# A graph network's second layer: relation rows made where they are used, operands read from PSUM, and puts that do not wait for each other

## The chip, the cores and the metric

The kernel runs on one NeuronCore of a Trainium2 chip. Its engines each work through a queue of their own: TensorE (PE; its weight loads are shown as PEld), VectorE (DVE), ScalarE (ACT), GpSimd (POOL) and SyncE (SP), with DMA transfers issued from several of these queues. The metric is device time in microseconds for one execution of the whole program, and lower is better. The kernel before took 3470.16 us, the median of nine runs that lay between 3455.51 and 3485.51.

## The reference

A graph has 3125 nodes with 256 features and 53125 edges (25000 drawn, each in both directions, and a self loop per node). Every edge has one of 64 types and a weight. The network has two layers, each followed by a feed-forward part with routing. Cut to what matters (L is a layer norm without scale; `W`, `b` are different for every place):

```python
xn = L(x)
# layer 0: weighted sum over neighbours, and a linear-attention "mixer"
x = x + segment_sum(xn[src] * w[:, None], dst) @ W.T + b + mixer0(xn)
# feed-forward 0: one of 32 experts for each node, by the largest logit
x = x + experts32(L(x))
# layer 1: attention over edges, with a row for each edge type
xn = L(x)
Q, K, V = heads(xn + 0.1 * query_emb)                 # 4 heads of 64
s  = einsum('ehd,ehd->eh', Q[dst], K[src] + 0.2 * rel_w[type][:, None, :]) / 8
a  = segment_softmax(s, dst)
out = segment_sum(a[:, :, None] * V[src], dst) @ Wo + bo
x = x + (L(out + xn) * gamma + beta) + mixer1(xn)
# mixer 1: 4 heads of 32; context = softmax(k over nodes)^T v; out = (q context) @ W_out + b_out
# feed-forward 1: a small graph attention gives 4 scores for each node;
# the two best of 4 experts are mixed
x = x + top2_of_4(L(x))
```

## The kernel before

The nodes are sorted by the number of their edges and cut into 25 tiles of 128 rows. Row p of a tile has one node, and its edges lie in slots: tile t has `SLOTS[t]` of them, from 38 down to 10, 444 in all. The source rows of a slot, one for each of the 128 nodes, are fetched by one indirect DMA (a gather) that GpSimd writes descriptors for. The residual `xs` stays in SBUF for all 25 tiles.

The code is written with tiles and pools. A pool has a number of buffers for each name, and a tile that takes a buffer waits for the readers of the one that had it before. The order in which an engine works through its instructions is set by a planner when the program is built, from the modelled readiness of each instruction; within `tc.manual_schedule(engines=...)` the named engines keep the order in which the program is written.

`layers()` (from L1675) holds both layers:

- `front()` (L1469) has layer 0 and the first half of layer 1. It prepares the edges, runs the first mixer over 25 tiles (`first_mixer`, L1368), then goes through seven groups of up to four tiles. For each tile, `slots` (L1341) gathers the neighbours' rows (L1351), weights and adds them on VectorE (L1357), and multiplies the sum by the layer's weights. `relation_rows` (L1311) then makes the row of `0.2 * rel_w[type]` for each slot: for four slots at a time VectorE writes a one-hot of the types (L1321), TensorE transposes two slots at once (L1327), ScalarE copies that to SBUF (L1329), TensorE multiplies it by the table in three bf16 parts (L1333), ScalarE copies the result to SBUF (L1336) and SP stores it in DRAM (L1338). After the four tiles come the 32 experts (`experts`, L1571: matmuls L1583, L1584 and L1588, activations L1586) and `projections` (L1601): keys and values of each tile are scattered to a DRAM table `kvtab` by node (L1619, on GpSimd), the layer-normed row and the query go to a DRAM table `own` (L1622, on SP), the second mixer's query goes transposed into `qT`, which is one half of the tile `kq` (L1626), and the mixer's context is summed up.
- `source_lists()` (L1221) scatters, in 256 DMAs of GpSimd (L1230), lists that the router will use.
- The second mixer's outputs are made for all 25 tiles one after the other (L1716 to L1720): two matmuls each into PSUM, and an add into `xs` on VectorE.
- The second layer's loop (L1725 to L1870) goes over the tiles. `scores(t)` loads `own` into `xq` (L1732) and the tile's relation rows into `rr` (L1734), and for each group of four slots has four gathers of 2 KB rows of keys and values from `kvtab` (L1742), then VectorE adds the relation rows to the keys (L1748), multiplies by the query (L1750) and sums over each head (L1751). A softmax over the slots follows (L1754 to L1763). `values(t)` weights the values, mostly on ScalarE by head (L1779) and for every fourth slot on VectorE (L1776), and TensorE sums them in PSUM by products with the identity (L1781). The gathers have 14 buffers of four slots. `project` (L1784) works one tile behind: it multiplies by the output weights and adds `xn` (L1791). After every five tiles, `norms` (L1841) adds to `xs`, and `router_rows` (L1806) makes the router's 20 numbers for each node and scatters them into a DRAM table (L1833).
- `routed_by_slots()` (L1893) is the last feed-forward part: gathers of 20 numbers for each node and each neighbour (L1910 and L1943), attention over them, gates, the four experts on TensorE (L2070 and L2082), adds into `xs` (L2101) and the puts of the tiles to the output by node, one indirect DMA each (`put`, L2104 to L2106). ScalarE, VectorE and GpSimd are in written order here.

Of the kernel before, what the change touches and what calls it, by code (L numbers as in the profile page):

```python
# [12 lines left out]
F32 = mybir.dt.float32  # L13
BF16 = mybir.dt.bfloat16
I32 = mybir.dt.int32
AF = mybir.ActivationFunctionType
OP = mybir.AluOpType
# [4 lines left out]
P = 128  # L22
N = 3125
D = 256
KB = D // P
NT = 25
# [870 lines left out]
class Fast(Net):  # L897
# [395 lines left out]
    def relations(self, ctx):  # L1293
        nc, a = self.nc, self.a
        HD, NR = 64, 64
        keep = ctx.enter_context(self.tc.tile_pool(name="rel_keep", bufs=1, reuse_waits="tile"))
# [14 lines left out]
    def relation_rows(self, pool, ps, t):  # L1311

        nc = self.nc
        HD, NR = 64, 64
        S = SLOTS[t]
        S2 = S + S % 2
        tab = self.dram.tile([P, S, HD], F32, name=f"rel{t}")
        for g in range(0, S2, 4):
            n = min(4, S2 - g)
            oh = pool.tile([P, 4, NR], BF16, name="oh")  # L1320
            nc.vector.tensor_tensor(  # L1321
                oh[:, :n], self.iota[:, None, :NR].to_broadcast([P, n, NR]),
                self.typs[t][:, g:g + n].unsqueeze(2).to_broadcast([P, n, NR]), op=OP.is_equal)
            po = ps.tile([P, 2, P], BF16, name="pg")
            ohT = pool.tile([P, 2, P], BF16, name="ohT")
            for i in range(n // 2):
                nc.tensor.transpose(po[:, i, :], oh[:, 2 * i:2 * i + 2, :].rearrange("p i r -> p (i r)"),  # L1327
                                    self.identb)
            nc.scalar.copy(ohT[:, :n // 2], po[:, :n // 2])  # L1329
            pr = ps.tile([P, 4, HD], F32, name="pg")  # L1330
            for i in range(n // 2):
                for k in range(3):
                    nc.tensor.matmul(pr[:, 2 * i:2 * i + 2, :], ohT[:, i, :], self.relb[:, k],  # L1333
                                     start=(k == 0), stop=(k == 2))
            rr = pool.tile([P, 4, HD], F32, name="rr")
            nc.scalar.copy(rr[:, :n], pr[:, :n])  # L1336
            n = min(n, S - g)
            nc.sync.dma_start(tab[:, g:g + n, :], rr[:, :n])  # L1338
        self.rels.append(tab)

    def slots(self, t, ep, eps, w_y):  # L1341
# [18 lines left out]
        both = eps.tile([P, 2, D], F32, name="sums")  # L1360
# [108 lines left out]
    def front(self, kq, kvtab, own):  # L1469
# [5 lines left out]
        with ExitStack() as ctx:  # L1475
# [6 lines left out]
            self.relations(ctx)  # L1482
# [7 lines left out]
            with ExitStack() as mctx:  # L1490
                self.first_mixer(mctx, kq, nq, kvo)
# [739 lines left out]
```

## Time and profile before

| what | us |
|---|---|
| median of nine runs | 3470.16 |
| the profiled execution | 3466.32 |
| its span on the core | 3464.4 |
| preparation | 0 to 100 |
| first mixer | 100 to 600 |
| groups of tiles with gathers | 600 to 1105 |
| the remaining groups, and the second mixer's outputs from 1943 | 1105 to 1981 |
| the loop's gathers | 1932 to 2697 |
| end of the loop, last part of the router's numbers | 2697 to 2773 |
| router and its experts | 2773 to 3421 |
| the last puts | 3421 to 3464 |

The stages overlap, and the bounds were read from the timeline. The mean granted clock of TensorE was 0.757 of full speed. "Busy" is the time in which an instruction ran on an engine; a group's line has its busy time, the mean in ns of one, the idle time of the engine just before its instructions, and what ended most of that. "issue" means that the profile shows nothing that the engine waited for. In a timeline, each line has start, duration, engine, source line and operation, and in brackets the idle time before it.

### The profile page before, as it was taken

What the parts mean: (1) busy time and instruction counts of PE and PEld (TensorE: products, weight loads), DVE (VectorE), ACT (ScalarE), POOL (GpSimd) and SP (SyncE); (2) the same over time, 40 slices, a digit from 0 to 9 for tenths busy, and PEclk for the clock granted to TensorE, in tenths of its full rate; (3) what the DMA queues carried; (4) which work ended last, traced back from release to release, by engine and by line L of the source; (5) the groups of instructions that cost most, each with busy time, mean ns of one, the idle gap of its engine ahead of it and who ended that gap; (6) DMA issues with size and microseconds to landing.
All of it is one profiled execution on the core that took longest, in us unless ns stands there. A gap on an engine that the chain in (4) does not pass through costs nothing. (4 is left out here: it accounts for less than half of the span.)

```text
span 3464.4 us, 25978 instructions
## 1 busy us (share of the span) xinstructions
PE 1977.0 (57%) x7293; PEld 1169.9 (34%) x7293; DVE 1389.1 (40%) x4121; ACT 902.3 (26%) x2670; POOL 1692.6 (49%) x1675
## 2 busy tenths in 40 slices
PE   0266676656657828466484615445556543865774
PEld 0134343333434414233242313233333322532443
DVE  7356566746633101111102355668668401111124
ACT  0023233112202201111011025456456511321230
POOL 3564544464362070513416177778777274455422
PEclk9977787777777969778595657667576665987887
DMA  3333323433232000000000255666676210000001
GB/s 119 119 97 97 92 90 102 156 107 116 74 94 67 21 22 10 25 0 25 1 12 13 76 164 175 190 199 198 196 214 188 91 29 5 17 12 7 11 6 37
DMA packets 142407, 283.68 MB, mean 82 GB/s; under 512 B 39826, under 2 KB 79750, under 8 KB 141868
## 3 DMA queue, kind: packets, MB, share of 16 engines
q0 software_dynamic: 82656, 196.67, 20.1%
q1 hardware_dynamic: 51340, 77.01, 6.5%
q10 hardware_dynamic: 8256, 8.23, 0.8%
q8 instruction: 61, 1.00, 0.1%
q14 instruction: 94, 0.77, 0.1%
HBM read 243.47 MB, written 38.31 MB: 81 GB/s over the span
## 5 line engine op out<-in xcount | busy, mean ns | idle before, releaser
L1351 POOL DMA_INDIRECT g<-xtab,src x444 | 452.6, 1019 | 421.9 <-issue 117.1
L1742 POOL DMA_INDIRECT kv<-kvtab,src x444 | 532.3, 1199 | 192.8 <-issue 159.4
L1781 PE MATMUL pu<-kv,ident 128*128 128x256 f32 x888 | 318.1, 505 | 252.2 <-ACT kv L1779 217.5
L1943 POOL DMA_INDIRECT ed<-htab,nb x279 | 264.7, 949 | 271.3 <-issue 177.0
L1779 ACT ACTIVATE kv<-kv,sc 128x64 f32<-128x64 f32 x1372 | 340.9, 335 | 147.4 <-DVE sc L1763 72.7
L1781 PEld LDWEIGHTS pu<-kv,ident 128*128 128x128 f32 x888 | 193.9, 245 | 364.4 <-ACT kv L1779 298.5
L1588 PE MATMUL po<-w,h 128*128 128x256 f32 x800 | 227.0, 429 | 155.2 <-ACT h L1586 143.4
L1230 POOL DMA_INDIRECT gl<-gsrc,sidx x256 | 248.6, 971 | 79.5 <-issue 77.5
L1619 POOL DMA_INDIRECT kvtab<-kv,pid x25 | 24.3, 973 | 531.4 <-DVE kv L1616 519.8
L2082 PE MATMUL po<-w,h 128*128 128x256 f32 x800 | 212.6, 406 | 105.7 <-issue 105.1
L2070 PE MATMUL ph<-xT,w 128*128 128x512 f32 (+1 forms) x448 | 199.2, 597 | 50.1 <-ACT h L2072 25.7
L1588 PEld LDWEIGHTS po<-w,h 128*128 128x128 f32 x800 | 158.5, 210 | 201.4 <-ACT h L1586 167.6
L1583 PE MATMUL ph<-xT,w 128*128 128x512 f32 (+1 forms) x448 | 211.8, 600 | 0.0
L1748 DVE TENSOR_TENSOR kv<-kv,rr 128x1024 f32<-128x1024 f32 (+3 forms) x121 | 136.3, 1129 | 185.9 <-DMA kv<-kvtab,src 165.8
L2082 PEld LDWEIGHTS po<-w,h 128*128 128x128 f32 x800 | 155.9, 200 | 156.7 <-issue 139.9
L1357 DVE SCALAR_TENSOR_TENSOR acc<-g,wt,acc 128x256 f32<-128x256 f32 x419 | 196.3, 475 | 18.4 <-DMA g<-xtab,src 12.3
L1586 ACT ACTIVATE h<-ph,b 128x512 f32<-128x512 f32 (+1 forms) x112 | 71.9, 642 | 500.5 <-PE ph L1584 358.3
L2070 PEld LDWEIGHTS ph<-xT,w 128*128 128x128 f32 x448 | 86.7, 207 | 147.4 <-issue 103.5
L1750 DVE TENSOR_TENSOR kv<-kv,xq 128x1024 f32<-128x1024 f32 (+3 forms) x121 | 134.8, 1124 | 0.1
L1751 DVE TENSOR_REDUCE sc<-kv 128x16 f32<-128x1024 f32 (+3 forms) x121 | 134.2, 1119 | 0.1
L2072 ACT ACTIVATE h<-ph,b 128x512 f32<-128x512 f32 (+1 forms) x112 | 69.1, 641 | 204.2 <-PE ph L2070 136.5
L1321 DVE TENSOR_TENSOR oh<-iota,typ 128x256 bf16<-128x256 f32 (+1 forms) x121 | 48.3, 401 | 178.4 <-PE pg L1327 116.6
(432 smaller groups left out, 3144.8 us busy)
## 6 DMA issues: line engine op xcount, KB each, us to landing
dr<-in_gat_dst_row SPq DMA_DIRECT2D x32, 512.0 KB
rel<-rr SPq DMA_DIRECT2D x101, 128.0 KB
g<-xtab,src POOLq DMA_INDIRECT x444
kv<-kvtab,src POOLq DMA_INDIRECT x444
own<-xq SPq DMA_DIRECT2D x25, 256.0 KB
xq<-own SPq DMA_DIRECT2D x25, 256.0 KB
ed<-htab,nb POOLq DMA_INDIRECT x279
w<-in_ex_w ACTq DMA_DIRECT2D x2, 2048.0 KB
```

What stands on the lines that cost most here:

```text
L1230: ins = nc.gpsimd.indirect_dma_start(out=self.gl[:, :], out_offset=bass.IndirectOffsetOnAxis(ap=self.sidx2[:, c:c + 1], axis=0), in_=self. ...
L1351: nc.gpsimd.indirect_dma_start(out=g[:, s % 4, :], out_offset=None, in_=self.xtab[:, :], in_offset=bass.IndirectOffsetOnAxis(ap=self.srcs[ ...
L1357: nc.vector.scalar_tensor_tensor(acc, g[:, s % 4, :], self.wts[t][:, s:s + 1], acc, op0=OP.mult, op1=OP.add)
L1583: nc.tensor.matmul(ph[:, :n], w1[:, k, mc], xT[:, k, :n], start=(k == 0), stop=False)
L1588: nc.tensor.matmul(pos[j // 2][:, j % 2], h[:, j * P:(j + 1) * P], w2[:, m, :], start=False, stop=(m == M - 1 and (j % 2 == 1 or j == w - 1)))
L1742: nc.gpsimd.indirect_dma_start(out=kv[:, j, :], out_offset=None, in_=kvtab[:, :], in_offset=bass.IndirectOffsetOnAxis(ap=self.srcs[t][:, g ...
L1748: nc.vector.tensor_tensor(k4, k4, rr[:, g:g + n].unsqueeze(2).to_broadcast([P, n, 4, HD]), op=OP.add)
L1779: nc.scalar.activation(v[:, h * HD:(h + 1) * HD], v[:, h * HD:(h + 1) * HD], AF.Copy, scale=sc[:, s, h:h + 1])
L1781: nc.tensor.matmul(pu, self.ident, v, start=(s == 0), stop=(s == SLOTS[t] - 1))
L1943: nc.gpsimd.indirect_dma_start(out=ed[:, s, :], out_offset=None, in_=self.htab[:, :], in_offset=bass.IndirectOffsetOnAxis(ap=self.nbrs[t][ ...
L2070: nc.tensor.matmul(ph[:, :w], w1[:, e, k, m * P:(m + 1) * P], xT[:, :len(ts), k, :], start=(k == 0), stop=(k == KB - 1))
L2082: nc.tensor.matmul(po[:, i], hs[i][:, m, j * P:(j + 1) * P], w2[:, e0 + i, m, :], start=False, stop=(i == 1 and m == M - 1))
```

## The change

Eight things are changed.

1. `relation_rows` is taken out of `front()` and called inside `scores(t)`, for eight slots at a time. Its result stays in PSUM (`pr`, two buffers), and VectorE reads it there. The copy `rr` on ScalarE, the DRAM tables `rel` and their stores and loads go.
2. The query is copied by ScalarE to a PSUM tile `q`, and VectorE's product reads it there.
3. The second mixer's output of a tile is made in `project`, into a second half of `pz`, with an add of its own into `xs`. `qT` is now a tile of its own that lives on; the first mixer's `q2T` has another. The mixer's weights and the relation table are loaded ahead of `front()`.
4. The PSUM pool of the loop has one buffer for each name, and two for `q`, `pr` and `pu`. `sums` in `slots` has two.
5. The router's numbers are made after 5, 10, 15, 20, 23 and 25 tiles, where it was every five.
6. In `routed_by_slots`, GpSimd's order is left to the planner.
7. The puts are declared independent of each other.
8. The scratch memory for the descriptors of dynamic DMAs is set to 4096, where it had its default.

```diff
-    def relation_rows(self, pool, ps, t):
+    def relation_rows(self, pool, ps, t, g):
...
-        for g in range(0, S2, 4):
-            n = min(4, S2 - g)
-            oh = pool.tile([P, 4, NR], BF16, name="oh")
...
-            rr = pool.tile([P, 4, HD], F32, name="rr")
-            nc.scalar.copy(rr[:, :n], pr[:, :n])
-            n = min(n, S - g)
-            nc.sync.dma_start(tab[:, g:g + n, :], rr[:, :n])
-        self.rels.append(tab)
+        n = min(8, SLOTS[t] + SLOTS[t] % 2 - g)
+        oh = pool.tile([P, 8, NR], BF16, name="oh")
+        nc.vector.tensor_tensor(
+            oh[:, :n], self.iota[:, None, :NR].to_broadcast([P, n, NR]),
+            self.typs[t][:, g:g + n].unsqueeze(2).to_broadcast([P, n, NR]), op=OP.is_equal)
+        pt = ps.tile([P, 4, P], BF16, name="pT")
+        ohT = pool.tile([P, 4, P], BF16, name="ohT")
+        for i in range(n // 2):
+            nc.tensor.transpose(pt[:, i, :], oh[:, 2 * i:2 * i + 2, :].rearrange("p i r -> p (i r)"),
+                                self.identb)
+        nc.scalar.copy(ohT[:, :n // 2], pt[:, :n // 2])
+        pr = ps.tile([P, 8, HD], F32, name="pr", bufs=2)
+        for i in range(n // 2):
+            for k in range(3):
+                nc.tensor.matmul(pr[:, 2 * i:2 * i + 2, :], ohT[:, i, :], self.relb[:, k],
+                                 start=(k == 0), stop=(k == 2))
+        return pr
...
-        both = eps.tile([P, 2, D], F32, name="sums")
+        both = eps.tile([P, 2, D], F32, name="sums", bufs=2)
...
-                    self.relation_rows(ep, eps, t)
...
-                kq = one.tile([P, KB, NP], F32, name="kq")
-                self.front(kq, kvtab, own)
+                q2T = one.tile([P, KB, NP], F32, name="q2T")
+                self.front(q2T, qT, kvtab, own)
...
-                    for t in range(NT):
-                        po = ps.tile([P, D], F32, name="pk")
-                        nc.tensor.matmul(po, qT[:, t * P:(t + 1) * P], cw, start=True, stop=False)
-                        nc.tensor.matmul(po, self.ones3, b_mo, start=False, stop=True)
-                        nc.vector.tensor_add(self.xs[:, t, :], self.xs[:, t, :], po)
...
-                    rr = ep.tile([P, S0, HD], F32, name="rr")
-                    nc.sync.dma_start(rr[:, :S], self.rels[t])
+                    q = ps.tile([P, D], F32, name="q", bufs=2)
+                    nc.scalar.copy(q, xq[:, :D])
...
+                        if g % 8 == 0:
+                            rr = self.relation_rows(ep, ps, t, g)
+                        r0 = g % 8
...
-                            k4, k4, rr[:, g:g + n].unsqueeze(2).to_broadcast([P, n, 4, HD]), op=OP.add)
-                        nc.vector.tensor_mul(k, k, xq[:, None, :D].to_broadcast([P, n, D]))
+                            k4, k4, rr[:, r0:r0 + n].unsqueeze(2).to_broadcast([P, n, 4, HD]), op=OP.add)
+                        nc.vector.tensor_mul(k, k, q[:, None, :].to_broadcast([P, n, D]))
...
-                    pz = ps.tile([P, D], F32, name="pz")
-                    self.mm_rows(pz, uT, w_o, b_o)
-                    nc.vector.tensor_add(z, xq[:, D:], pz)
+                    pz = ps.tile([P, 2, D], F32, name="pz")
+                    self.mm_rows(pz[:, 0], uT, w_o, b_o)
+
+                    nc.tensor.matmul(pz[:, 1], qT[:, t * P:(t + 1) * P], cw, start=True, stop=False)
+                    nc.tensor.matmul(pz[:, 1], self.ones3, b_mo, start=False, stop=True)
+                    nc.vector.tensor_add(z, xq[:, D:], pz[:, 0])
+                    nc.vector.tensor_add(self.xs[:, t, :], self.xs[:, t, :], pz[:, 1])
...
+                parts = [range(a0, b0) for a0, b0 in zip((0, 5, 10, 15, 20, 23), (5, 10, 15, 20, 23, 25))]
...
-                engines={mybir.EngineType.Activation, mybir.EngineType.DVE, mybir.EngineType.Pool}))
+                engines={mybir.EngineType.Activation, mybir.EngineType.DVE}))
...
+                if puts:
+                    tc.declare_no_dep(ins, group="out", reason="other nodes")
+                tc.add_to_no_dep_group("out", ins)
+                puts.append(t)
...
-    nc = bacc.Bacc("TRN2", target_bir_lowering=False, num_devices=1)
+    nc = bacc.Bacc("TRN2", target_bir_lowering=False, num_devices=1, dynamic_dma_scratch_size=4096)
```

## The prediction

> **What bounds the kernel now.** I read the busy shares first, then the busy time by stretch, then the costliest groups, the waits, the chain that ended last, and the timelines of GpSimd and VectorE where the loop begins.
>
> The page's shares and granted clock:
>
> ```profile
> span 3464.4 us, 25978 instructions
> PE 1977.0 (57%) x7293; PEld 1169.9 (34%) x7293; DVE 1389.1 (40%) x4121; ACT 902.3 (26%) x2670; POOL 1692.6 (49%) x1675
> ```
>
> No engine is the bound of the whole, so it goes by stage. The stretches are: first mixer, two tile groups with gathers, five groups without, the second layer's loop, its end, the router with its experts, the tail. Columns: us, then busy time and count of PE, PEld, DVE, ACT, POOL, then clock, DMA share, GB/s.
>
> ```profile
> 100.00:600.00 500.00, 295.85 (x1437) 174.81 (x1438) 282.25 (x1131) 132.83 (x400) 256.02 (x254) 0.79 0.34 102
> 600.00:1105.00 505.00, 307.16 (x1499) 187.98 (x1498) 270.33 (x1028) 96.38 (x232) 253.77 (x250) 0.77 0.34 106
> 1105.00:1935.00 830.00, 502.03 (x1684) 281.01 (x1684) 108.42 (x351) 120.97 (x271) 268.45 (x301) 0.78 0.05 17
> 1935.00:2697.00 762.00, 393.76 (x1143) 239.58 (x1143) 486.51 (x792) 357.13 (x1373) 562.78 (x473) 0.66 0.61 182
> 2697.00:2773.00 76.00, 45.09 (x152) 28.79 (x152) 37.71 (x89) 39.44 (x152) 11.54 (x10) 0.72 0.24 77
> ```
>
> In front TensorE leads with 59 to 61% busy. In the loop it is GpSimd: 562.8 of 762 us in descriptor writing alone, and each gather is followed by a gap of 0.30 us (444 x 0.30 = 133 us), together 696. The groups:
>
> ```profile
> L1742 POOL DMA_INDIRECT kv<-kvtab,src x444 | 532.3, 1199 | 192.8 <-issue 159.4 <-ACT kv L1779 16.6 <-PE pu L1781 5.2
> L1327 PE MATMUL pg<-identb,oh 128*128 128x128 bf16 x229 | 37.2, 245 | 120.6 <-issue 73.4 <-ACT rr L1336 42.8 <-DVE oh L1321 2.9
> L1333 PE MATMUL pg<-self.relb,ohT 128*128 128x128 bf16 x687 | 69.2, 238 | 34.6 <-ACT ohT L1329 14.2 <-remote 12.0 <-issue 4.6
> L1336 ACT COPY rr<-pg 128x256 f32<-128x256 f32 (+1 forms) x121 | 43.8, 362 | 223.6 <-remote 100.7 <-PE pg L1333 59.9 <-issue 27.9
> ```
>
> A gather alone takes 0.95 us. The timelines show what stretches it: one that starts beside L1748, an add of two operands in SBUF, takes 1.94; and the second gather buffer came only when the last L1720 of the second mixer was done, after 43.97 us.
>
> ```profile
> 2206.01 1.22 DVE L1748 TENSOR_TENSOR kv<-kv,rr 128x1024 f32<-128x1024 f32 x1 [2.27 <-DMA kv<-kvtab,src]
> 2206.11 1.94 POOL L1742 DMA_INDIRECT kv<-kvtab,src  x1 [0.30 <-issue]
> ...
> 2217.03 0.95 POOL L1742 DMA_INDIRECT kv<-kvtab,src  x1 [0.30 <-issue]
> ...
> 1980.57 0.42 DVE L1720 TENSOR_TENSOR xs<-xs,pk 128x256 f32<-128x256 f32 x1 [1.05 <-PE pk L1719]
> ...
> 1980.95 1.99 POOL L1742 DMA_INDIRECT kv<-kvtab,src  x1 [43.97 <-issue]
> ```
>
> The tail, by the chain that ended last and the timeline: the last adds end near 3421, then puts to the output run one after the other, each waiting until the one before has landed.
>
> ```profile
> 3419.67 0.39 issue
> 3420.06 3.28 DMA out<-xs,pid
> ...
> 3436.81 0.96 POOL L2106 DMA_INDIRECT out<-xs,pid  x1 [2.21 <-DMA out<-xs,pid]
> 3459.11 0.96 POOL L2106 DMA_INDIRECT out<-xs,pid  x1 [2.21 <-DMA out<-xs,pid]
> ```
>
> **The sum's base** is the profiled execution: 3466.3 us, of which 3464.4 is span and 1.9 lies around it. The median of nine runs is 3470.2, 0.1% above; no change under about 0.3% can be told from none.
>
> **Front, relation rows out: -55 (0 to -150).** Gone are 229 transposes and 687 matmuls (37.2 + 69.2 = 106 us of TensorE), 121 one-hots (48.3 us of VectorE), two copies a group on ScalarE (43.9 + 43.8) and 101 stores on SP. TensorE is busy about 0.6 of these stages, and the small matmuls were often filling gaps, so I count half of the 106: 53, and 2 for the copies in TensorE's way. At 0, other work sets the pace: the gathers L1351 (452.6 us busy) or the chain of the experts hides it all. At most, 106 plus L1336's 44: 150.
>
> **Second mixer into the loop: -44 of GpSimd's start.** Its 50 matmuls (30.2 us) and 25 adds (10.4 at 415 ns, as L1791) no longer stand between the projections and the loop. The gathers start at 1936 and need not wait until 1981: 44 us. The work itself lies in project(), where TensorE is half idle. If the buffer waits for another owner of that memory instead, 0.
>
> **VectorE reads PSUM: -86 on GpSimd (0 to -111).** 444 gathers x (1.199 - 0.95) = 111 us is the stretch. Laid over VectorE's instructions, the gathers that met only L1751, with one input, took 949 ns mean, only reads of PSUM 960, only L1750 1674. With rows and query in PSUM both two-input operations become of the first kind. I leave 25 us of stretch for L1776, the one-hots and the softmax, whose inputs stay in SBUF. At 0, the stretch is from any long VectorE operation. VectorE itself gains or loses nothing: 256 wide from SBUF and PSUM, L1791 took 414 ns, L1776 415. [...]
>
> **What the loop gets: +60 of that back.** VectorE: 67 one-hots of 512 elements at about 0.62 (L1321's 401 ns for 256, extrapolated) = 42, on 486: 528. ScalarE: 25 query copies x 0.37 and 67 copies x 0.59 (L1165's 512 wide) = 49, on 357: 406. TensorE: 106 on 394: 500. SP loses 25 loads of rows. GpSimd: 444 x 1.25 = 555, 25 of stretch, 25 table scatters and 16 list gathers at about 1.3 = 54: 634. So GpSimd stays the longest, but its margin over the chain shrinks: each chunk of eight slots has one-hot, transposes, copy, matmuls before its first L1748, and these queue on TensorE behind the matmuls L1781 (which wait 217.5 us for ScalarE) and on ScalarE behind 335-ns products L1779. I take a third of the 155 us given to TensorE and ScalarE, about 52, and 8 for single-buffered PSUM, as path. The ends are 0 (hidden) and +270 (67 chunks x 4 us, all exposed: one-hot 0.6, four transposes of 37.2/229 = 0.16, copy 0.6, twelve matmuls of 69.2/687 = 0.10, together 3.0, and 1 for the hand-offs between engines). Loop: 44 + 86 - 60 = **-70**, from 765 to about 695.
>
> **Last router part of two tiles: -8.** From norms at 2745 to the first router gather at 2773.7 is 29 us; of the five table scatters (2760.3 to 2768.0) three go earlier, 5 us, and 3 of normalising.
>
> **Puts without the wait: -37.** The last add ends at 3421, the last put starts at 3459.1; with nothing to wait for it starts near 3421.7. Only if the adds came later is there less to win. **Free POOL order and 4096 of scratch: 0** (order: ±10, GpSimd idles 53% of the router stage; scratch: up to four gathers were in flight at once in the loop, a price as a rival).
>
> Sum: -55 - 70 - 8 - 37 = -170, **3296**.
>
> **Rival 1: the loop gives nothing.** The chunks' chains are exposed: 528 + 270 = 798 us of VectorE instead of 765, +33. For it: VectorE already waits 165.8 us for gathers and lags 25 us at the end; TensorE waits behind L1781. Against: the one-hots depend on nothing in the loop and rows have two buffers. -55 + 33 - 8 - 37 = -67: about 3400.
>
> **Rival 2: TensorE becomes the loop's bound, slower.** 916 matmuls and as many weight loads more: some eight more 16-KB loads of code (13 to 21) in a stage where the clock is 0.66. Each cost about 3 us of TensorE's "issue" time there (42 for 13); while GpSimd issues back to back in the router stage, one matmul of 0.59 us came every 2.80. At 17 us a code load, 500 + 357 = 857: +95, and front gives 30 only: +95 - 30 - 8 - 37 = +20, **3486**. It decides from a loop of about 840 on; below it the case is rival 1. Against: 1143 matmuls went through 762 us with 394 busy.
>
> **Rival 3: the small scratch makes GpSimd wait** for landings. The latency of a gather is 3.4 us median; if 1 in 28 of 1614 DMAs waits one latency, 58 x 3.4 = 197: -170 + 197 = +27. Against it only that no more than four were in flight; it needs a wait every 28th, and shows as gaps regular on GpSimd.
>
> **How the numbers follow.** Forecast 0.62, rival 1 0.25, rivals 2 and 3 together 0.11, nothing at all 0.02. Low end: front -110, loop -115 (GpSimd alone, 650), -8, -37 = -270: 3196, say 3200. High end: rival 1 with 20 more, 3420. The forecast's own range is 3230 to 3350. Faster: 0.62 + 0.25 = 0.87; same 0.02; slower 0.11.
>
> **What the profile after would show.** Gathers L1742's successor at 0.95 to 1.0 mean instead of 1.199 (else the PSUM step is wrong); the first wait of 44 us gone; loop about 695; no rr copies; the puts 1.3 us apart; front's stages some 55 shorter in all. Wrong it is if VectorE's add waits for the row matmuls (rival 1), if TensorE's idle in the loop is mostly "issue" (rival 2), or GpSimd shows waits on its own landings (rival 3).

## The result and the profile after

The changed kernel takes 3701.6 us (median of ten runs), the kernel before beside it 3472.3: a ratio of 1.067, 95% interval 1.065 to 1.070. The forecast was 0.95 and the range ended at 3420 us.

Runs of this study fell on chips of two kinds. On some the kernel before takes 3470 to 3504 us, as here; on others it takes 2782 to 2794. I call them the first and the second kind; the name says how a chip behaved in these runs, and whether it always does was not tried. Each ratio compares runs on one and the same chip, and on the second kind the changed kernel has 1.003. Of the distance from the forecast 0.95 to the measured 1.067, about half (0.064) thus came with the first kind of chip, and the other half (0.053) is in the kernel on either.

The profiled execution after has a span of 3681.2 us, before 3464.4. Its page, and the busy time by stretch (us, then PE, PEld, DVE, ACT, POOL, then clock, DMA share, GB/s; the stretches are those shown of before, cut where the loop's gathers now begin and end, from the groups without gathers on):

```profile
span 3681.2 us, 25500 instructions
PE 2012.3 (55%) x7293; PEld 1184.0 (32%) x7293; DVE 1385.4 (38%) x4071; ACT 870.2 (24%) x2520; POOL 1573.8 (43%) x1675
```

```profile
1105.00:1909.00 804.00, 478.93 (x1437) 262.53 (x1435) 92.41 (x295) 101.64 (x206) 266.37 (x298) 0.77 0.04 12
1909.00:2898.00 989.00, 455.98 (x1926) 290.68 (x1926) 489.86 (x809) 383.11 (x1430) 455.02 (x474) 0.65 0.43 126
2898.00:3025.00 127.00, 69.03 (x287) 44.64 (x287) 71.87 (x142) 53.88 (x191) 10.65 (x11) 0.67 0.11 37
```

The gathers begin at 1909 instead of 1932, 23 us earlier. They take 989 us instead of 765, though VectorE's work is the same (490 and 487 us) and GpSimd's fell from 563 to 455: no engine is busy for half of the stretch. From the first gather of the loop to the first gather of the router, which I call the loop from here on, it is 1116 us after and 841 before. What follows takes 656 instead of 691. With the span, -23 + 275 - 35 = +217, which is the whole difference.

The groups of the loop after:

```profile
L1731 POOL DMA_INDIRECT kv<-kvtab,src x444 | 426.2, 960 | 501.0 <-ACT kv L1768 375.0 <-issue 109.8 <-PE pu L1770 6.4
L1737 DVE TENSOR_TENSOR kv<-kv,pr 128x1024 f32<-128x1024 f32 (+3 forms) x121 | 133.4, 1124 | 335.2 <-remote 264.2 <-PE pr L1329 30.9 <-PE pT L1323 29.6
L1325 ACT COPY ohT<-pT 128x512 bf16<-128x512 bf16 (+3 forms) x67 | 34.8, 519 | 282.6 <-remote 207.6 <-PE pT L1323 59.7 <-issue 10.8
```

The gathers' mean is 960 ns, down from 1199: that step did what was forecast. But GpSimd stands 375 us waiting for buffers that ScalarE's products L1768 have still to work on, and VectorE's add waits 335 us for its rows. 264 of these end as "remote": the profile finds no instruction whose end let it go. The timeline shows what that means:

```profile
2275.74 0.56 ACT L1325 COPY ohT<-pT 128x512 bf16<-128x512 bf16 x1
2276.75 0.83 PE L1329 MATMUL pr<-self.relb,ohT 128*128 128x128 bf16 x12
2277.42 0.28 PE L1323 MATMUL pT<-identb,oh 128*128 128x128 bf16 x2
2277.57 0.95 POOL L1731 DMA_INDIRECT kv<-kvtab,src  x1 [0.30 <-issue]
...
2286.07 0.37 ACT L1775 COPY u<-pu 128x256 f32<-128x256 f32 x1 [9.77 <-remote]
...
2295.11 0.94 POOL L1731 DMA_INDIRECT kv<-kvtab,src  x1 [0.30 <-issue]
2300.08 2.35 DVE L1737 TENSOR_TENSOR kv<-kv,pr 128x1024 f32<-128x1024 f32 x2 [30.06 <-remote]
2300.20 0.37 ACT L1325 COPY ohT<-pT 128x256 bf16<-128x256 bf16 x1 [13.76 <-remote]
```

By the records TensorE has made the rows and the next transposes by 2277.7 us. ScalarE's copy of the sums starts 8 us later, VectorE's add and the copy of the transposes 22 us later, 4 us after the last of GpSimd's gathers. Until then the two engines do nothing but that one copy of the sums. Laying all such waits over GpSimd's work (rows of eight or more DMAs less than 0.6 us apart, together 1916 of 3681 us): of 788 us in which VectorE's waits end as "remote", 690 lie in such rows and 770 in them or within 5 us after; of ScalarE's 892 us, 755 and 865. The rows with their 5 us make up 2185 us, 59% of the span, and hold 98 and 97% of these waits. On the other kind of chip no view of the same program shows a wait that ends as "remote".

The puts at the end no longer wait for landings but, most of them, for the adds:

```profile
3674.09 0.98 POOL L2101 DMA_INDIRECT out<-xs,pid  x1 [0.36 <-DVE xs L2096]
3676.04 0.96 POOL L2101 DMA_INDIRECT out<-xs,pid  x1 [0.97 <-DVE xs L2096]
```

### The profile page after: what moved, and what is told of

Same layout as the page of the kernel before. It is cut to its first block, busy times and chain, and to the rows that moved or that the text cites. A ratio compares the mean times of both kernels' runs of the same rounds, so it can differ in the third digit from the quotient of the medians.

```text
span 3681.2 us, 25500 instructions
## 1 busy us (share of the span) xinstructions
PE 2012.3 (55%) x7293; PEld 1184.0 (32%) x7293; DVE 1385.4 (38%) x4071; ACT 870.2 (24%) x2520; POOL 1573.8 (43%) x1675
## 5 line engine op out<-in xcount | busy, mean ns | idle before, releaser
L1731 POOL DMA_INDIRECT kv<-kvtab,src x444 | 426.2, 960 | 501.0 <-ACT kv L1768 375.0
L1343 POOL DMA_INDIRECT g<-xtab,src x444 | 444.0, 1000 | 395.2 <-issue 117.7
L1770 PE MATMUL pu<-kv,ident 128*128 128x256 f32 x888 | 297.1, 478 | 166.8 <-ACT kv L1768 141.1
L1768 ACT ACTIVATE kv<-kv,sc 128x64 f32<-128x64 f32 x1372 | 333.6, 334 | 63.9 <-DVE sc L1752 44.2
L1770 PEld LDWEIGHTS pu<-kv,ident 128*128 128x128 f32 x888 | 178.8, 228 | 276.2 <-ACT kv L1768 221.2
L1737 DVE TENSOR_TENSOR kv<-kv,pr 128x1024 f32<-128x1024 f32 (+3 forms) x121 | 133.4, 1124 | 335.2 <-remote 264.2
L1577 ACT ACTIVATE h<-ph,b 128x512 f32<-128x512 f32 (+1 forms) x112 | 71.9, 642 | 538.7 <-PE ph L1575 384.1
L1329 PE MATMUL pr<-self.relb,ohT 128*128 128x128 bf16 x687 | 75.0, 284 | 191.5 <-ACT ohT L1325 146.0
L1739 DVE TENSOR_TENSOR kv<-kv,q 128x1024 f32<-128x1024 f32 (+3 forms) x121 | 133.4, 1122 | 0.1
L1582 DVE SCALAR_TENSOR_TENSOR xs<-po,xs 128x256 f32<-128x256 f32 x25 | 9.4, 416 | 327.1 <-PE po L1579 326.8
```

The costliest lines, as they stand in the source:

```text
L1343: nc.gpsimd.indirect_dma_start(out=g[:, s % 4, :], out_offset=None, in_=self.xtab[:, :], in_offset=bass.IndirectOffsetOnAxis(ap=self.srcs[ ...
L1731: nc.gpsimd.indirect_dma_start(out=kv[:, j, :], out_offset=None, in_=kvtab[:, :], in_offset=bass.IndirectOffsetOnAxis(ap=self.srcs[t][:, g ...
L1737: nc.vector.tensor_tensor(k4, k4, rr[:, r0:r0 + n].unsqueeze(2).to_broadcast([P, n, 4, HD]), op=OP.add)
L1768: nc.scalar.activation(v[:, h * HD:(h + 1) * HD], v[:, h * HD:(h + 1) * HD], AF.Copy, scale=sc[:, s, h:h + 1])
L1770: nc.tensor.matmul(pu, self.ident, v, start=(s == 0), stop=(s == SLOTS[t] - 1))
```

## Experiments

The chip's kind is given by the kernel before beside the run. "Late" is VectorE's idle time in the loop, in waits longer than 1 us, that ended as "remote" or "issue" (nothing that the profile shows).

| kernel | kind | ratio to before, 95% | loop, us | late, us |
|---|---|---|---|---|
| before | first | 1 | 841 | 43 |
| changed | first | 1.067 (1.065 to 1.070) | 1116 | 347 |
| late_dma | first | 1.062 (1.056 to 1.068) | 1102 | 323 |
| hots_tile | first | 1.058 (1.045 to 1.072) | 1094 | 282 |
| hots_front | first | 0.986 (0.979 to 0.993) | 866 | 173 |
| rows_psum_act_4 | first | 0.998 (0.995 to 1.002) | 898 | 150 |
| plain_loads_3 | first | 0.983 (one run) | 835 | 0 |
| before_puts | second | 0.986 (0.981 to 0.991) | 813 | 9 |
| after_again | second | 1.003 (1.001 to 1.005) | 852 | 3 |
| pr3 | second | 0.998 (0.996 to 1.000) | 838 | 3 |
| rows_sbuf | second | 1.004 (1.001 to 1.007) | 857 | 5 |
| mixer_out | second | 1.011 (1.008 to 1.013) | 872 | 0 |
| plain_loads, plain_loads_2 | second | 1.003 (1.000 to 1.006), 1.000 (0.998 to 1.002) | 827, 828 | 0 |
| rows_front | second | 0.974 (0.970 to 0.977) | 779 | 13 |
| rows_front_qsbuf | second | 0.972 (0.970 to 0.974) | 771 | 13 |
| hots_front_2 | second | 0.936 (0.930 to 0.943) | 691 | 3 |
| rows_psum_act, _2, _3 | second | 0.937 (0.936 to 0.939), 0.938 (0.933 to 0.942), 0.932 (0.926 to 0.938) | 683, 679 (_1, _3) | 2 |

**The puts alone.** The kernel before, with the puts independent, and with GpSimd's order in the router stage left to the planner, which the first needs.

```diff
+                if puts:
+                    tc.declare_no_dep(ins, group="out", reason="other nodes")
+                tc.add_to_no_dep_group("out", ins)
+                puts.append(t)
...
-                engines={mybir.EngineType.Activation, mybir.EngineType.DVE, mybir.EngineType.Pool}))
+                engines={mybir.EngineType.Activation, mybir.EngineType.DVE}))
```

> The kernel before, with only the puts declared independent and GpSimd's order in the router stage left to the planner, which the first needs. The prediction's term was -37 us: ratio near 0.989. If the planner's freer order costs something in the router stage, less than that is left; if the puts were hidden by something else, 1.00.

0.986, that is (1 - 0.9862) x 2785 = 38 us less (24 to 53 by the interval). This step of the prediction holds. Its loop, which is that of before, serves as the loop of before on the second kind: 813 us.

**Rows back in front.** The old `relation_rows` in front; the loop loads its result from DRAM.

```diff
                     self.slots(t, ep, eps, w_y)
+                    self.relation_rows(ep, eps, t)
...
                         if g % 8 == 0:
-                            rr = self.relation_rows(ep, ps, t, g)
+                            n8 = min(8, S - g)
+                            rr = ep.tile([P, 8, HD], F32, name="rr", bufs=5)
+                            nc.sync.dma_start(rr[:, :n8], self.rels[t][:, g:g + n8])
```

(For want of memory in front, the mixer's small weights are loaded after it and one buffer there is single; so too in the kernels below that make something in front.)

> The changed kernel with the relation rows made in front again, stored to DRAM and loaded for eight slots at a time into SBUF; the query stays in PSUM and the second mixer's outputs stay in the loop. Theory A, that the chain VectorE - TensorE - ScalarE - TensorE of the rows sits on the path of the loop: the loop (first gather to first router gather) falls from 1116 us to 760 to 820, the front takes some 20 more, ratio to the kernel before 0.96 to 0.99. Theory B, that the single-buffered PSUM tiles and the second mixer's outputs in project couple the tiles whatever the rows do: the loop stays above 1000, ratio above 1.04.

0.974, and the loop is 779 us against 852 for the changed kernel on the same kind of chip. Theory A's numbers came out, though they were meant for a fall from 1116 us: here the loop fell from 852. The front did not get longer: the loop's gathers begin at 1472 us here, at 1484 in the changed kernel and at 1485 in before_puts. On this kind of chip, taking the rows out of the front was worth nothing.

**How far ahead the rows can be made.** Copies to five SBUF buffers, or three PSUM buffers:

```diff
-                            rr = self.relation_rows(ep, ps, t, g)
+                            pr = self.relation_rows(ep, ps, t, g)
+                            n8 = min(8, S - g)
+                            rr = ep.tile([P, 8, HD], F32, name="rr", bufs=5)
+                            nc.scalar.copy(rr[:, :n8], pr[:, :n8])
```

> The changed kernel, rows made in the loop as there, but ScalarE copies each chunk's rows from PSUM to one of five SBUF buffers, so that rows can be made up to seven chunks ahead of VectorE instead of two. Theory A': the chain hurts because it can run only two chunks ahead: the loop falls from 1116 to about 850 to 950, ratio 1.00 to 1.03. Theory A'': it hurts because ScalarE and TensorE serve it late, however far ahead: the loop stays within 50 us, ratio 1.05 to 1.08, a little more for 67 copies more on ScalarE (0.6 us each, 40 us).

```diff
-        pr = ps.tile([P, 8, HD], F32, name="pr", bufs=2)
+        pr = ps.tile([P, 8, HD], F32, name="pr", bufs=3)
...
-                    q = ps.tile([P, D], F32, name="q", bufs=2)
+                    q = ps.tile([P, D], F32, name="q", bufs=1)
```

> The changed kernel with three row buffers in PSUM instead of two, and one query buffer instead of two. Theory A' (the look-ahead of two chunks is what hurts): the loop falls by 50 to 120 us, ratio 1.03 to 1.05. Theory A'' (served late): within 20 us of the changed kernel, ratio 1.06 to 1.075.

Loops of 857 and 838 us against 852. More room to run ahead does almost nothing on this kind, so A' falls here: the rows are served late, not held back for want of buffers. rows_sbuf alone would not show it, for VectorE reads the rows from SBUF there and the gathers go from 974 to 1075 ns, 45 us in all; pr3 leaves them in PSUM. The ratios that I gave were for the first kind of chip and say nothing here, and on that kind A' was not tried.

**The changed kernel again, on the second kind.** No edit.

> The changed kernel, unaltered, beside the others. The chip of the last four runs took 2785 us for the kernel before, where the chip of the result took 3472. Theory C: what the change loses is the lateness of TensorE's hand-offs on the first chip (VectorE's add waited up to 59 us for rows whose matmuls were long done); on a chip like the second, where these waits end with TensorE's work, the ratio is 0.99 to 1.01 and the loop about 840 us. Theory A (the chain itself is too long on any chip): ratio 1.03 to 1.07. If the chip is again like the first: 1.067, and C stays open.

1.003 and 852 us: theory C's numbers. The mean granted clock is 0.822 here and 0.744 on the first kind; what becomes of that difference is under "No descriptors from GpSimd". What is left of the loss here is visible in the timeline of this run:

```profile
1639.89 11.07 ACT L1768 ACTIVATE kv<-kv,sc 128x64 f32<-128x64 f32 x46
1640.63 0.22 PE L1323 MATMUL pT<-identb,oh 128*128 128x128 bf16 x1
1641.18 0.22 PE L1323 MATMUL pT<-identb,oh 128*128 128x128 bf16 x1
...
1650.87 0.56 ACT L1325 COPY ohT<-pT 128x512 bf16<-128x512 bf16 x1
1651.55 0.83 PE L1329 MATMUL pr<-self.relb,ohT 128*128 128x128 bf16 x12
...
1652.42 2.35 DVE L1737 TENSOR_TENSOR kv<-kv,pr 128x1024 f32<-128x1024 f32 x2 [10.29 <-PE pr L1329]
```

The transposes are done at 1641.4, but ScalarE's copy of them stands behind the products of the tile before (72 in a row, since 1633.7) and starts at 1650.9. Then all goes at once: the matmuls at 1651.6, the add at 1652.4, after 10.3 us of nothing for VectorE. Here the waits end with the work that they are for. By the records 14 of the 67 copies stand directly behind 40 or more products, up to 116, and 85 of the 96 us that the add waits for the rows come after such copies. On the first kind the add had 264 us of "remote" instead:

```profile
DVE kv L1737 <- PE pr L1329: 96.1, 18, 13.9
```

**The second mixer out of the loop again.**

```diff
+                    for t in range(NT):
+                        po = ps.tile([P, D], F32, name="pm", bufs=2)
+                        nc.tensor.matmul(po, qT[:, t * P:(t + 1) * P], cw, start=True, stop=False)
+                        nc.tensor.matmul(po, self.ones3, b_mo, start=False, stop=True)
+                        nc.vector.tensor_add(self.xs[:, t, :], self.xs[:, t, :], po)
...
-                    nc.tensor.matmul(pz[:, 1], qT[:, t * P:(t + 1) * P], cw, start=True, stop=False)
-                    nc.tensor.matmul(pz[:, 1], self.ones3, b_mo, start=False, stop=True)
-                    nc.vector.tensor_add(self.xs[:, t, :], self.xs[:, t, :], pz[:, 1])
```

> The changed kernel with the second mixer's 25 outputs made before the loop again, one after the other, from two PSUM buffers; rows stay in the loop. If the gathers wait for them as before, the loop begins some 40 us later and gains at most the 25 x (1.2 + 0.4) us of TensorE and VectorE back: ratio 0.01 above the changed kernel beside it. If it is their place in project that couples the tiles, the loop shortens by more than 40 us: ratio below it.

1.011 against 1.003, and 20 us more in the loop: VectorE's first add starts 36 us after the first gather instead of 8. So the mixer's place in `project` does not couple the tiles. The wait that the prediction priced at 44 us does not come back here, for the gathers do not wait for the mixer in this kernel (they start 1.3 us apart from the first on); this run prices the place of the work and not that wait. Theory B's other half, the single-buffered PSUM tiles, falls by the kernels below that keep them and have loops of 683 and 691 us.

**Rows and query from PSUM or SBUF, with the rows made in front.** Both edits are against rows_front; `rs` is what `rr` was there.

```diff
                             rs = ep.tile([P, 8, HD], F32, name="rs", bufs=5)
                             nc.sync.dma_start(rs[:, :n8], self.rels[t][:, g:g + n8])
+                            rr = ps.tile([P, 8, HD], F32, name="pr", bufs=2)
+                            nc.scalar.copy(rr[:, :n8], rs[:, :n8])
```

> Rows made in front and loaded from DRAM, as in rows_front, then copied by ScalarE to two PSUM buffers of eight slots, from which VectorE's add reads them. The gathers' mean falls from 1059 ns to about 970 (40 us of GpSimd), but one copy on ScalarE, in written order with the products, is on VectorE's path again. If only making the rows is too much for the path: ratio 0.96 to 0.97 on a chip like the last. If any hand-off from ScalarE in two buffers is: 0.98 to 1.00, VectorE's add waiting for ScalarE.

```diff
-                    q = ps.tile([P, D], F32, name="q", bufs=2)
-                    nc.scalar.copy(q, xq[:, :D])
+                    q = xq[:, :D]
```

> rows_front with VectorE's product reading the query from SBUF again and no copy of it to PSUM. The gathers' mean rises from 1059 ns back to about 1180 (444 x 0.12 = 53 us of GpSimd): ratio 0.985 to 0.995 where rows_front had 0.9735. If stretched gathers cost nothing because something else sets the loop's pace: 0.97 to 0.975.

The gathers of the three, query in SBUF, then query in PSUM, then both in PSUM (third run of that kernel):

```profile
L1742 POOL DMA_INDIRECT kv<-kvtab,src x444 | 519.2, 1169 | 145.1 <-issue 108.2 <-ACT kv L1779 16.1 <-DMA kv<-kvtab,src 7.0
```

```profile
L1743 POOL DMA_INDIRECT kv<-kvtab,src x444 | 470.1, 1059 | 186.0 <-issue 104.2 <-ACT kv L1780 58.1 <-DMA kv<-kvtab,src 8.2
```

```profile
L1745 POOL DMA_INDIRECT kv<-kvtab,src x444 | 428.3, 965 | 144.4 <-issue 97.2 <-ACT kv L1782 22.0 <-DMA kv<-kvtab,src 12.8
```

1169, 1059, 965 ns: each operand moved to PSUM takes about 100 ns off a gather, as the forecast had it. The query alone is worth nothing (0.974 with it in PSUM, 0.972 without): the idle time before the gathers grows by as much. With both the loop is 683 us, 88 below rows_front_qsbuf, for 444 x 0.204 = 91 us of descriptor writing. Why the first half of that gave nothing and the second all of it, no run shows; the order of the instructions, planned anew for each kernel, may have part in it. Against the loop of before, 813, rows_front_qsbuf has 771: 42 us for the mixer, the router's parts and the PSUM pool together. The two steps make 130 us, which is what the prediction had put down to the earlier start and the unstretched gathers, 44 + 86. So close an agreement is partly luck: the 44 was read on the first kind, and on the second that wait is 33.9 us in before_puts.

rows_psum_act says one thing more. It has 67 copies on ScalarE in the loop, each between a load and VectorE's add, in two buffers, and its loop is the shortest of all. Both readings that I had given for it were too slow. A copy on ScalarE did not cost much by itself here: none of their waits is put down to a load, and only 5 of the 67 stand directly behind 40 or more products.

**One hop more in the chain** (on the first kind):

```diff
-        nc.scalar.copy(ohT[:, :n // 2], pt[:, :n // 2])
+        ohA = pool.tile([P, 4, P], BF16, name="ohA")
+        nc.scalar.copy(ohA[:, :n // 2], pt[:, :n // 2])
+        nc.sync.dma_start(ohT[:, :n // 2], ohA[:, :n // 2])
```

> The changed kernel with one hop more in each chunk's chain: the transposed one-hots go from ScalarE's copy through an SBUF-to-SBUF transfer of SP before TensorE reads them. It takes no time of TensorE, ScalarE or VectorE, only some 2 to 3 us of lateness a chunk. If the lateness of the rows sets the loop's pace (theory C: on the first chip hand-offs came 5 to 30 us late), 67 chunks x 2.5 us = 170 us at most, and I expect half of it or more on the loop: 85 to 170 us, ratio 1.03 to 1.06 on a chip where the changed kernel has 1.003. If the chain has slack and the work on the engines is what costs: under 20 us, ratio under 1.01.

1.062: no loss at all beside 1.067. By the records the first row matmul now starts 3.1 us (median) after ScalarE's copy, where it was 0.06. A few microseconds of lateness at this place cost nothing on this kind; in this form my theory C falls. That what costs is being held for 10 to 30 us at a time, or behind a whole tile's products, fits the timelines; this run does not show it.

**One-hots and transposes in front, matmuls in the loop.**

```diff
-        nc.scalar.copy(ohT[:, :n // 2], pt[:, :n // 2])
+        ohT = pool.tile([P, 4, P], BF16, name="ohT", bufs=5)
+        nc.sync.dma_start(ohT[:, :n // 2], self.rels[t][:, g // 2:(g + n) // 2, :])
         pr = ps.tile([P, 8, HD], F32, name="pr", bufs=2)
```

> The changed kernel with the first half of the chain moved back: one-hots, their transposes and ScalarE's copy are made in front and stored to DRAM; the loop loads them and keeps only the 687 matmuls, whose result VectorE reads from PSUM. If TensorE's matmuls, in order behind the sums L1770, are the late step: loop about 800 to 850, ratio 0.99 to 1.00. If the late steps are VectorE's one-hot and ScalarE's copy: loop about 690, as with the rows copied to PSUM by ScalarE, ratio 0.94 to 0.95.

> The kernel with one-hots and transposes made in front and only the 687 matmuls in the loop, for a second chip if this is one. Where the kernel before takes 2785: if VectorE's one-hot and ScalarE's copy were the late steps, loop about 690 and ratio 0.94 to 0.95; if TensorE's matmuls behind the sums L1770 are, about 0.99 to 1.00. Where it takes 3470: 0.986 again.

On the first kind 866 us for the loop and 0.986, on the second 691 and 0.936. The 687 matmuls, whose result VectorE still takes straight from PSUM, are cheap on the second kind; the one-hot, the transposes and ScalarE's copy in front of them together cost 250 us on one kind and 161 on the other. Of the 161, 39 are VectorE's own work, which leaves the loop (556 us busy against 518), and 122 are idle time. That answers the question on the second kind as the second reading had it; on the first neither reading's numbers came.

**One-hot or copy?** One instruction makes a tile's one-hots:

```diff
+        if g == 0:
+            self.oh = pool.tile([P, 38, NR], BF16, name="oh")
...
+        oh = self.oh[:, g:g + n]
```

> The changed kernel with the one-hots of a whole tile made by one instruction (up to 38 x 64 wide) at the tile's start instead of one for each eight slots. Transposes, ScalarE's copy and matmuls stay in the loop, chunk by chunk. If VectorE's one-hot, in order behind the adds of the chunk before, is the late step: loop 700 to 760 us where the kernel before takes 2785, ratio 0.95 to 0.97. If ScalarE's copy behind the products L1768 is: within 30 us of the changed kernel's 852, ratio 0.99 to 1.01. Where the kernel before takes 3470: by the first 0.99 to 1.02, by the second 1.05 to 1.07.

1.058 and a loop of 1094 us, as expected on this kind if the transposes and ScalarE's copy, not VectorE's one-hot, are late. On the second kind it was not tried, so which of the three steps costs what there is read from the timeline alone.

**No descriptors from GpSimd.** The changed kernel with plain loads by SP. It leaves the gather out: the bytes are as many, but the keys and values are those of wrong nodes.

```diff
-                            nc.gpsimd.indirect_dma_start(
-                                out=kv[:, j, :], out_offset=None, in_=kvtab[:, :],
...
+                            r0_ = (t + g + j) % NT * P
+                            nc.sync.dma_start(kv[:, j, :], kvtab[r0_:r0_ + P, :])
```

> The changed kernel in which the loop's 444 gathers are replaced by plain loads of 128 consecutive rows of the same table, issued by SP: the same bytes, but GpSimd writes no descriptors for them. It leaves the gather out, so keys and values are those of wrong nodes. Theory D: on a chip with the late hand-offs (kernel before near 3470) TensorE is held up while GpSimd writes descriptors back to back. Then in the loop nearly all of the waits that end by a late hand-off go (788 us on VectorE and 892 on ScalarE in the whole program, about 350 of VectorE's in the loop), and the loop falls from 1116 to about 800 to 870, what the same program takes on the other chip (852). Rival E: TensorE is late there whatever GpSimd does (power, code loading): the loop stays above 1000. On a chip like the second (2785) only the gathers' own time goes: loop 750 to 850.

> The changed kernel with plain loads by SP in place of the loop's 444 gathers (wrong nodes' keys and values; the gather is left out). On a chip where the kernel before takes about 2785 this was 1.003, as the changed kernel is. On a chip with late hand-offs (3470): theory D, that TensorE is held up while GpSimd writes descriptors back to back, expects the loop to fall from 1116 to 800 to 900 us and VectorE's waits for late hand-offs in it to nearly nothing, ratio 0.97 to 1.00. Rival E, that TensorE is late there whatever GpSimd does: loop above 1000, ratio above 1.03.

> The changed kernel with plain loads by SP in place of the loop's 444 gathers (wrong nodes' keys and values; the gather is left out). On a chip with late hand-offs (kernel before 3470): theory D, that TensorE is held up while GpSimd writes descriptors back to back, expects the loop to fall from 1116 to 800 to 900 us and VectorE's waits for late hand-offs in it to nearly nothing. Rival E, that TensorE is late there whatever GpSimd does: loop above 1000. On a chip with 2785: 1.00, as twice before.

Twice it ran on the second kind, where the ratio stayed and the loop lost 25 us (827 and 828 against 852): there the gathers do little to set the loop's pace. The third, one run on the first kind, tells D from E. The loop falls from 1116 to 835 us, and no late wait is left in it. VectorE's waits in the loop, of the changed kernel and then of this one:

```profile
DVE kv L1737 <- remote: 264.2, 14, 59.0
DVE kv L1737 <- PE pr L1329: 30.9, 13, 5.9
```

```profile
DVE kv L1735 <- PE pr L1329: 85.7, 16, 13.9
DVE kv L1735 <- DMA kv<-kvtab: 31.9, 4, 10.7
```

With GpSimd nearly silent (25 of 835 us busy), the loop of the first kind is that of the second, to 1%: 835 and 828. The granted clock in it is 0.74 on both, where the changed kernel had 0.65 on the first kind and 0.72 on the second, so the lower clock goes with the late waits and is no fixed mark of the chip. Outside the loop, where GpSimd still writes, the late waits remain (517 us on VectorE). Of the 281 us that the loop lost, some 25 would have gone on the second kind too. So the gathers that GpSimd issues back to back are the cause of the late hand-offs in the loop; rival E falls. Loads of code, which E and the prediction's rival 2 had in mind, are not: the loop has 19 of them in the changed kernel on either kind and here, and TensorE's idle time that ends as "issue" in it is 152, 2 and 0 us. The edit takes out the writing of descriptors and the transfers that follow from it at once. Which of the two does it was not shown: that it is the writing is my guess, and the ends of the waits do not settle it (of VectorE's 46 "remote" waits over 5 us in the profile after, 26 end within a row of eight or more of GpSimd's DMAs, 20 outside). Nor does any run show by what way GpSimd's work reaches TensorE.

**A chain without TensorE, on the first kind.** Unaltered kernels, for the other kind of chip.

> The kernel with rows made in front and copied by ScalarE from SBUF to two PSUM buffers, unaltered from the run before, for a second chip if this is one. Its chain in the loop has no TensorE in it. Theory D: on a chip with late hand-offs it loses little more than the kernel before does there: ratio 0.93 to 0.96, loop 680 to 760. If other hand-offs are late too: 0.97 to 1.00. On a chip like the second: 0.937 again.

> Rows made in front, copied by ScalarE from SBUF to two PSUM buffers; no TensorE in the rows' chain in the loop. Where the kernel before takes 3470, theory D expects a ratio of 0.93 to 0.96 and a loop of 680 to 760 us, below the 866 of the kernel that keeps the 687 matmuls in the loop; if hand-offs of ScalarE are late there too, 0.97 to 1.00. Where it takes 2785: 0.937 again.

> Rows made in front, copied by ScalarE from SBUF to two PSUM buffers; no TensorE in the rows' chain in the loop. Where the kernel before takes 3470, theory D expects a ratio of 0.93 to 0.96 and a loop of 680 to 760 us, below the 866 of the kernel that keeps the 687 matmuls in the loop; if hand-offs of ScalarE are late there too, 0.97 to 1.00. Where it takes 2785: 0.93 to 0.94 again.

Two runs were on the second kind and gave 0.938 and 0.932. On the first it is 0.998 with a loop of 898: not theory D's numbers, but in the range of the reading that other hand-offs are late too. The waits there:

```profile
ACT u L1789 <- remote: 82.3, 8, 25.3
ACT kv L1782 <- issue: 80.7, 96, 13.0
```

```profile
DVE z L1797 <- remote: 91.0, 9, 15.9
DVE kv L1751 <- PE pu L1784: 35.0, 2, 18.0
```

The rows are no longer what is waited for most. ScalarE's copy of the sums and VectorE's add of the projection are, both in `project`, both handed over by TensorE, and `project` was there before the change. Its lateness had cost the kernel before little (43 us on VectorE). In that kernel VectorE read two SBUF operands and gathers took 1199 ns; with gathers at 954 ns more is late. Whether slower descriptor writing leaves TensorE more room, or `project` merely had slack before, was not tried and stays open.

Of the versions, the one with one-hots and transposes in front and the matmuls in the loop is faster than both kernels on both kinds: 0.986 (0.979 to 0.993) and 0.936 (0.930 to 0.943). On the first kind that is little more than the puts give: its loop, 866 us, is not shorter than that of before, 841. No version that gathers had a shorter loop there than before.

## Why the prediction was wrong

- **Front, -55.** The gathers began 23 us earlier on the first kind; on the second, rows in front or in the loop made no difference (1472 and 1484). The cheap end of the bounds was near. That the small matmuls filled gaps of TensorE, or that other work set the pace, as the lower bound said, fits this; which of them it was, no run shows.
- **Second mixer, -44.** Right in the main: the wait is gone, and VectorE's first add starts at 1931 instead of 1981. On the second kind, where the wait is 33.9 us, the loop got 42 us shorter by it together with the router's parts and the PSUM pool (813 to 771), and 20 us longer with the mixer ahead of the loop and no such wait.
- **VectorE reads PSUM, -86.** Right as a mechanism and in its size on GpSimd: 1199 to 960 ns after, 1169 to 1059 to 965 in steps, and on the second kind 88 us of the loop (on the first no loop got shorter). VectorE's add took 1129 ns with the rows in SBUF before and 1124 with them in PSUM after, so VectorE itself neither gained nor lost, as forecast. But in the changed kernel the step freed GpSimd, which was not what the new loop waited for.
- **What the loop gets, +60 of that back.** This step failed. By the prediction's own terms the loop on the second kind should have been 813 - 130 = 683; the kernels with the late steps taken out reach 683 and 691, the changed one 852. So 169 us were given back where 60 were forecast. On the first kind, 1116 - (841 - 130) = 405, beyond the upper end of 270. Of these, 250 go with the one-hots, transposes and copies (866 us without them); the other 155 stay, in a loop with 173 us of late waits. I had priced a chunk's chain by the durations of its instructions, with 4 us at most. Two prices were missing. ScalarE's copy stands behind up to a tile's products in a fixed order (68 in 16.3 us in one place of the profile after); on the second kind 85 of the add's 96 us of waits come after such copies. And on the first kind hand-offs come late beside GpSimd's rows of DMAs: 690 of VectorE's 788 us of "remote" waits and 755 of ScalarE's 892 lie in these rows, which are 52% of the span after.
- **Last part of two tiles, -8.** Not tried by itself. The time from the last gather to the router grew from 76 to 127 us, so whatever it gave was lost.
- **Puts, -37.** Right: what follows the loop is 35 us shorter in the result, and 38 us (24 to 53) came by itself.
- **The rivals.** Rival 1 had the place right (VectorE's add waits for the rows) and the price wrong: +33 for the loop, where it was +275. Rival 2 had the other sign right: its row, one matmul of 0.59 us every 2.80 while GpSimd issues back to back (first line below), was the sign of what came, but I tied it to code loads and to TensorE's own pace instead of to whoever waits for TensorE. Its 17 us a code load came from no row; the 19 loads in the changed loop, against 12 before, left TensorE 2 us of "issue" on the second kind. That its 3486 is nearer than the forecast is luck. Rival 3 falls: GpSimd waits 4 us in all for its gathers' own landings.

Of the profile of before, a line of its timeline and one of its groups:

```profile
2855.63 0.59 PE L2082 MATMUL po<-w,h 128*128 128x256 f32 x1 [2.21 <-issue]
```

```profile
L1329 ACT COPY ohT<-pg 128x256 bf16<-128x256 bf16 (+1 forms) x121 | 43.9, 363 | 129.2 <-PE pg L1327 55.3 <-remote 51.3 <-issue 7.0
```

The evidence for the first kind's part was in the profile of before: "remote" and "issue" stood as releasers in the lines of the copies L1336 and L1329 (100.7 and 51.3 us of "remote") and of the transposes L1327 (73.4 us of "issue"). In front these waits cost little, for nobody needed the rows soon. I moved the chain, in my sum, with its busy time and without its waits.

## What to carry to other kernels

The chain of small hand-offs, cheap off the path, took its waits along when it was moved (100.7 us of "remote" before the copy L1336 in front, 264.2 before VectorE's add in the loop). Price such a chain by its idle time and releasers where it stands, and by what stands in the fixed order of each engine where it goes. Where a wait ends by nothing that the profile shows, look for what another engine does at that time (here 98% of VectorE's lay in GpSimd's rows of DMAs or in the 5 us after), before tying work of a hot loop to the engine that is late. Of a chain that must move, leave behind the steps that hand over from engine to engine between long rows of other work. On the second kind the 687 matmuls could come into the loop for next to nothing (691 us), and so could 67 copies on ScalarE whose input was there early (683 us). What could not come was the one-hot, the transposes and the copy between them: made just in time, the copy stood behind a tile's products.

## What the runs showed of the hardware

In the changed kernel on the first kind of chip TensorE was late while GpSimd issued DMAs back to back, with its own instructions as with what it hands over: of 570 us of TensorE's idle time that ended as "issue", 546 lie in GpSimd's rows of eight or more DMAs (52% of the span), beside the 690 of 788 and 755 of 892 us of "remote" on VectorE and ScalarE. In the router's stage of the changed kernel, on the first and then on the second kind of chip, the same program:

```profile
L2077 PE MATMUL po<-w,h 128*128 128x256 f32 x800 | 207.6, 403 | 83.4 <-issue 83.1
```

```profile
L2077 PE MATMUL po<-w,h 128*128 128x256 f32 x800 | 187.8, 387 | 0.0
```

83 us of idle time that nothing in the profile explains, against none; 69 of the 83 lie in rows of eight or more of GpSimd's DMAs. In all, the two kinds differ by 3472 to 2785 us for the kernel before. Taking GpSimd's gathers out of the loop took 281 us off it on the first kind and 25 on the second; so on the first TensorE or its signals do wait there, by whatever way.
